# Group norm, attention and projection on one core: chains of the projections in row halves of the array, score units one at a time between their steps, products with v in lumps

## The chip, the core and the metric

The kernel runs on one core of a Trainium2 chip. The metric is the device time of one execution in microseconds (us): two runs of the kernel before gave 1596.97 and 1597.28, median 1597.12. The engines of the core are named as in its profile: PE (matrix multiply), PEld (its weight loads), DVE (vector), ACT (scalar, here mostly the exponential), POOL and SP (which issues most transfers). Each engine works through its own list in order; a wait in the list holds up everything behind it.

## What is computed

The input x is (4, 512, 48, 48): four batches (b), 512 channels, 2304 positions. The reference, cut to what matters (d is 64, 8 heads):

```python
hn = _group_norm(x, gn_scale, gn_bias)            # 32 groups
qkv = einsum('oc,bchw->bohw', qkv_w, hn) + qkv_b  # to float16, heads of 64
w = softmax(einsum('bhct,bhcs->bhts', q * scale, k * scale))
a = einsum('bhts,bhcs->bhct', w, v)
out = x + einsum('oc,bchw->bohw', proj_w, a) + proj_b
```

## The kernel before

Two heads of a batch form a pair; there are 16 pairs, g = 0 to 15. The 2304 queries are cut into five blocks j, four of 512 and one of 256. For one pair and block the work is a row of **score units**: a unit is k times q for 128 keys and 512 queries of both heads (two matmuls of 64 rows by 128 columns side by side in the two row halves of the array, one head each; line 1066), written to a slot of two PSUM banks, and one exponential of 128x1024 on ACT (L1073), which writes 16-bit numbers to SBUF. Three units are a step (BURST); there are 432 steps in all and 1296 units. The **product with v** (L1091) takes the exponentials two steps later: two matmuls of 128 rows by 64 columns, side by side in the two column halves, for each unit, summed in the PSUM bank av. DVE adds the exponentials of the steps up (L1122, L1127); PE sums them over the keys with a matrix of ones (sl, L1150), and the quotient goes through a small transfer to DRAM and back (L1169, L1197, L1207).

Beside this runs the rest of the work as **chains**, sums over the 512 channels in one PSUM bank that DVE empties at the end: pqk (q and k of coming pairs, L802, 32-bit, column halves), pv (v, L854, the same) and pr (output projection, L948, whole array, with weights split into a high and a low part). A 32-bit matmul appears in the trace as two instructions. The lists beside (chains waiting, each with the step at which it is needed) and fill (which after each step issues half a chain to a chain and a half, by how much must be done until when) set where chains stand. The main loop of fast_path writes, for each step: three score units, sums if a block ended, then chain pieces, then the product of the step two back. PSUM is split in three slots for scores, one bank for av and sl, one for chains.

Of the kernel before, what the change touches and what calls it, by code (L numbers as in the profile page):

```python
# [26 lines left out]
P = 128  # L27
# [6 lines left out]
BEHIND = 2  # L34
LAG = 2
# [435 lines left out]
def fast_path(  # L471
# [19 lines left out]
    apool = ctx.enter_context(tc.tile_pool(name="apool", bufs=2 * NPAIR - 1))  # L491
    ppool = ctx.enter_context(tc.tile_pool(name="ppool", bufs=3))
# [87 lines left out]
    share = const.tile([P, P // GROUP, GROUP], F32, name="share")  # L580
# [19 lines left out]
    def chain_bank(name):  # L600
        if alone[0]:
            return ps_s.tile([P, 2, QB], F32, tag="ps", name=name)[:, 0, :]
        return ps_w.tile([P, QB], F32, tag="pw", name=name)

    def small_bank(name):
        return ps_w.tile([P, QB], F32, tag="pw", name=name)
# [85 lines left out]
    def first_group(meanwhile):  # L692
# [5 lines left out]
        pv = ps_s.tile([P, 2, QB], F32, tag="ps", name="first_vars")[:, 0, 0:1]  # L698
# [59 lines left out]
    def piece(us, run, first=False, last=False, when=None):  # L758
        return [us, run, first, last, when, 0, NG]
# [16 lines left out]
    def idle_once(*engines):  # L776
        for engine in engines:
            if idle_left[engine] > 0:
                idle_left[engine] -= 1
                getattr(nc, engine).nop("place", nofuse=True)  # L780

# [47 lines left out]
    def qk_chain(g, part, j):  # L829
        n = QBLOCKS[j][1]  # L830
        steps = qk_steps(g, part, j)
        return chain_pieces(n / 600.0, steps, HALVES if n == QB else WHOLE)
# [4 lines left out]
    def v_chain(b, half, i):  # L837
# [31 lines left out]
        return chain_pieces(1.72, one, (range(1), range(1, 2)))  # L869
# [54 lines left out]
    def att32(b, j, pairs=range(NC), beside=None):  # L924
        o, n = QBLOCKS[j]
        for c in pairs:
# [10 lines left out]
            at32[b, j, c] = t[:, :n]  # L937
            source = atts[b * NPAIR + c][:, o : o + n]
# [45 lines left out]
    def proj_piece(b, j, chunks, pairs=range(NC), ahead=None):  # L984
        def run():
            evacuate, store = proj_run(b, j, chunks, pairs)
            evacuate()
            if pairs == LAST:
                finished.add((j, chunks[0]))

            if pairs != FIRST:
                loads.append((now[0] + 1, store))
            if ahead is not None:
                loads.append((now[0] + 1, ahead))

        return piece(QB / 290.0 * len(pairs) / NC, run, True, True)
# [55 lines left out]
    def scores(u, ahead_of_last=None):  # L1052
        g, j, k, _ = u
        o, n = QBLOCKS[j]
        per = QB // n
        qt, kt = qk[g]
        pt = ppool.tile([P, BURST, 2, QB], F16, tag="p", name=f"p_{g}_{j}_{k}")
        for r in range(BURST):
            if r == BURST - 1 and ahead_of_last:
                ahead_of_last()  # L1060
            ps = ps_s.tile([P, 2, QB], F32, tag="ps", name=f"ps_{g}_{j}_{k}_{r}")
            for a in range(per):
                i = (k * BURST + r) * per + a
                for h in range(2):
                    rows = slice(h * D, (h + 1) * D)
                    nc.tensor.matmul(  # L1066
                        ps[:, h, a * n : (a + 1) * n],
                        kt[rows, bass.ts(i, P)],
                        qt[rows, o : o + n],
                        start=True,  # L1070
                        stop=True,
                    )
            nc.scalar.activation(pt[:, r], ps, AF.Exp)  # L1073
        pts[u] = pt

    def values(u):
        g, j, k, last = u
        b, pr = divmod(g, NPAIR)
        o, n = QBLOCKS[j]
        per = QB // n  # L1080
        pt = pts.pop(u)
        if k == 0:
            if j == 0:
                atts[g] = apool.tile([P, T], F16, tag="att", name=f"att_{g}")
            av[0] = ps_av.tile([P, QB], F32, tag="av", name=f"av_{g}_{j}")
        for r in range(BURST):
            for a in range(per):
                i = (k * BURST + r) * per + a
                for h in range(2):
                    lo = h * D  # L1090
                    nc.tensor.matmul(  # L1091
                        av[0][lo : lo + D, :n],
                        vv[b, pr // 2][:, i, pr % 2 * P + lo : pr % 2 * P + lo + D],
                        pt[:, r, h, a * n : (a + 1) * n],
                        start=(i == 0),
                        stop=(i == NT - 1),
                    )
        if last and u is not stream[-1]:
            avx[g, j] = work.tile([P, QB], F32, tag="avx", name=f"avx_{g}_{j}")
            nc.vector.tensor_copy(avx[g, j][:, :n], av[0][:, :n])  # L1100
# [3 lines left out]
    def add(u):  # L1104

        g, j, k, last = u
        pt = pts[u]
        if k == 0:
            acc[g, j] = [pt]
            return  # L1110
        if j >= NQ - 2 and g == NG - 1 and (last or j == NQ - 1):
            acc[g, j].append(pt)
            return
        before = acc[g, j][0]
        if k == 1:
            acc[g, j] = [
                work.tile(
                    [P, BURST, 2, QB], F16, tag="acc", bufs=1, name=f"acc_{g}_{j}"
                )
            ]  # L1120
        t = acc[g, j][0]
        nc.vector.tensor_tensor(t, before, pt, ALU.add)  # L1122
        if last:
            acc[g, j] = [t[:, :1]]

            def join(r):
                nc.vector.tensor_tensor(t[:, 0], t[:, 0], t[:, r], ALU.add)  # L1127

            for r in range(1, BURST - 1):
                join(r)  # L1130
            joins.append(lambda: join(BURST - 1))

    def add_up(g, j, bank=None, more=False):
# [5 lines left out]
        if bank is None:  # L1139
            sl = ps_av.tile([P, QB], F32, tag="av", name=f"sl_{g}_{j}")  # L1140
        steps = [
            (t, r, a)
            for t in acc.pop((g, j))
            for r in range(t.shape[1])
            for a in range(per)
        ]
        for i, (t, r, a) in enumerate(steps):
            for h in range(2):
# [4 lines left out]
                    t[:, r, h, a * n : (a + 1) * n],  # L1153
# [58 lines left out]
    def divide(g, j):  # L1212
        divided[0] = now[0]
        o, n = QBLOCKS[j]
# [10 lines left out]
    def put(pieces, after=0, need=NG):  # L1225
        for p in pieces:
            p[5], p[6] = after, need
        beside.extend(pieces)

    def put_run(run, *args, when=None, after=0):  # L1230

        put([piece(0.05, lambda: run(*args), when=when)], after)

# [36 lines left out]
    def copies_next():  # L1270

        return any(p[0] == 0.0 and p[5] <= now[0] for p in beside[:2])

    def put_qk(g, part, blocks=range(NQ)):

        for j in blocks:
            put(qk_chain(g, part, j), (g - 2) * per_pair - 1, g)

    def put_v(b, half, tiles=range(0, NT, 2)):
        for i in tiles:  # L1280
            g = b * NPAIR + 2 * half
            pieces = v_chain(b, half, i)
            last = (b, i * P // QB, NC - 1)
            if half == 0:
                pieces[0][4] = lambda last=last: normed.get(last, now[0]) < now[0]
            put(pieces, (g - 2) * per_pair + 1, g)

    ends = [i for i, u in enumerate(stream) if u[3]]
    projs = {(b, j): proj_pieces(b, j) for b in range(B) for j in range(NQ)}

# [6 lines left out]
    def put_convert(b, j):  # L1297
        end = ends[((b + 1) * NPAIR - 1) * NQ + j]
        put(projs[b, j][0], end + ready(b, j))

    def put_proj(b, j, ahead=None):

        end = ends[((b + 1) * NPAIR - 1) * NQ + j]
        for p in projs[b, j][1]:
            if ahead:
                put_run(*ahead.pop(0))
            put([p], end + ready(b, j) + 1)

    def put_first(b, j, ahead):

        for jj, chunks in proj_list:
            if jj == j:
                if ahead:
                    put_run(*ahead.pop(0))
                put([proj_piece(b, j, chunks, FIRST)])

    for b in range(B):
        g = b * NPAIR
        old = b - 1
        if b == 0:  # L1320
            for j in range(NQ):
# [4 lines left out]
                put_qk(g + 1, 1, (j,))  # L1326
                put_qk(g + 1, 0, (j,))
            for block in SPARE:
                put_run(reload, *block)
        put_qk(g + 2, 1)  # L1330
        put_qk(g + 2, 0)
# [6 lines left out]
        if b == B - 1:  # L1338
            put_qk(g + 3, 1)
            put_qk(g + 3, 0, range(NQ - 1))  # L1340
            put_convert(old, 0)
            put_qk(g + 3, 0, (NQ - 1,))

            THIRD = range(len(EARLY), NC - 1)
            ahead = [
                (residual, b, j, chunks)
                for j in (NQ - 2, NQ - 3, NQ - 1)
                for jj, chunks in proj_list
                if jj == j
            ]  # L1350
            ahead += [
                (att32, b, j, (c,)) for j in (NQ - 2, NQ - 3, NQ - 1) for c in EARLY
            ]
            ahead.append((att32, b, NQ - 2, THIRD))
            for j in range(NQ):
                put_proj(old, j, ahead)
                if j + 1 < NQ:
                    put_convert(old, j + 1)
            assert not ahead

            ahead = [
                (att32, b, NQ - 3, THIRD),
                (att32, b, NQ - 1, THIRD),
                *((att32, b, 0, (c,), True) for c in EARLY),
            ]
            for j in (NQ - 2, NQ - 3, NQ - 1):
                put_first(b, j, ahead if j != NQ - 2 else [])
# [8 lines left out]
        for j in early:  # L1376
            if j == NQ - 1 and b > 0:
                put_convert(old, 0)
            put_qk(g + 3, 1, (j,))
            put_qk(g + 3, 0, (j,))  # L1380
            put_run(reload, b + 1, j)
        for j in late:
            put_v(b, 1, tiles[j])
            put_qk(g + 3, 1, (j,))
            put_qk(g + 3, 0, (j,))
        if b > 0:
            for j in range(NQ - 1):
                put_proj(old, j)
                put_convert(old, j + 1)
        put_v(b + 1, 0)  # L1390
        if b > 0:
            put_proj(old, NQ - 1)
        put_qk(g + 4, 1)
        put_qk(g + 4, 0)
        put_qk(g + 5, 1)
        put_qk(g + 5, 0)
# [305 lines left out]
```

## Time and profile before

| | us |
|---|---|
| median of the two runs | 1597.12 |
| span of the profiled execution, first to last instruction | 1595.6 |
| PE busy | 1582.0 (99%) |
| ACT busy | 1269.4 (80%) |
| DVE busy | 1140.2 (71%) |

The page gives for the profiled execution the span of its instructions; the median of the runs lies 1.5 us above it. A group's row reads: line, engine, operation, tile written <- tiles read, shape, count | busy time in all, mean ns of one | idle time before them. Matmuls are pipelined: one lasts longer than the distance to the next, so distances between starts are read from the timeline, and a PE that shows as busy all the time may still lose time in switching between halves.

### The profile page before, as it was taken

How to read it: one execution, taken by the hardware profiler on the slowest of the kernel's cores; microseconds unless marked ns; L12 is line 12 of the kernel's file. 1: busy time of each engine (PE TensorE's matmuls, PEld its weight loads, DVE VectorE, ACT ScalarE, POOL GpSimd, SP SyncE). 2: the span in 40 equal slices, each digit the busy share in tenths (PEclk: the TensorE clock that was granted, in tenths of full speed). 3: DMA queues.
4: the chain of work that ended last, by engine and by line, in shares of the span. 5: the costliest groups of instructions: out<-in, count | busy, mean ns of one | idle time of the engine just before them, and what ended most of it. 6: DMA issues, size and time to landing. Idle time of an engine off the chain costs nothing. (4 is left out here: it accounts for less than half of the span.)

```text
span 1595.6 us, 28731 instructions
## 1 busy us (share of the span) xinstructions
PE 1582.0 (99%) x11526; PEld 701.7 (44%) x11526; DVE 1140.2 (71%) x1302; ACT 1269.4 (80%) x1363; POOL 336.8 (21%) x463
## 2 busy tenths in 40 slices
PE   9999999999999999999999999999999999999997
PEld 3733434443333534545333354455533334434554
DVE  6267668876666678887666666888767676767776
ACT  4177777888888888888888888887878888888885
POOL 1001202222121222312112121222212121121232
PEclk9999999999999999999999999999999999999999
DMA  7002020000000024521000001353101000015424
GB/s 222 3 14 67 12 73 16 18 14 12 15 18 11 12 69 119 144 67 28 11 14 18 14 12 41 111 158 88 23 17 18 15 15 11 15 31 166 149 62 133
DMA packets 94896, 82.10 MB, mean 51 GB/s; under 512 B 50852, under 2 KB 60964, under 8 KB 94756
## 3 DMA queue, kind: packets, MB, share of 16 engines
q1 hardware_dynamic: 92724, 78.35, 18.1%
q8 instruction: 92, 1.51, 0.4%
q10 hardware_dynamic: 1904, 1.84, 0.4%
q14 instruction: 48, 0.39, 0.1%
q0 software_dynamic: 128, 0.01, 0.0%
HBM read 60.70 MB, written 19.17 MB: 50 GB/s over the span
## 5 line engine op out<-in xcount | busy, mean ns | idle before, releaser
L1073 ACT ACTIVATE p<-ps 128x1024 f16<-128x1024 f32 x1296 | 1233.5, 1025 | 299.1 <-PE ps L1066 296.3
L1122 DVE TENSOR_TENSOR acc<-acc,p 128x3072 f16<-128x3072 f16 x270 | 485.4, 1798 | 53.8 <-ACT p L1073 51.3
L802 PE MATMUL pqk<-x,wqkv 128*64 128x512 f32 (+1 forms) x2432 | 510.3, 549 | 0.1
L1091 PE MATMUL av<-p,v 128*64 128x512 f16 (+1 forms) x2880 | 360.6, 364 | 0.0
L1066 PE MATMUL ps<-q,k 64*128 64x512 f16 (+1 forms) x2880 | 355.8, 358 | 0.4 <-DVE v L862 0.2
L854 PE MATMUL pv<-wqkv,x 128*64 128x256 f32 x2304 | 267.6, 379 | 0.3 <-DVE v L862 0.3
L802 PEld LDWEIGHTS pqk<-x,wqkv 128*64 128x64 f32 x2432 | 168.5, 137 | 205.4 <-issue 155.9
L1188 POOL TENSOR_SCALAR in<-sums 128x8 f32<-128x8 f32 (+1 forms) x158 | 100.8, 638 | 712.4 <-DMA sums<-slx 705.8
L1066 PEld LDWEIGHTS <-k 64*128 64x128 f16 x2880 | 105.9, 94 | 287.2 <-issue 238.2
L1091 PEld LDWEIGHTS <-v 128*64 128x64 f16 x2880 | 131.2, 109 | 212.8 <-issue 168.1
L1215 POOL TENSOR_TENSOR att<-avx,ib 128x512 f16<-128x512 f32 (+1 forms) x78 | 133.1, 1706 | 422.9 <-DMA ib<-row 373.7
L854 PEld LDWEIGHTS pv<-wqkv,x 128*64 128x64 f32 x2304 | 166.3, 137 | 81.3 <-DVE v L862 0.8
L1122 DVE TENSOR_TENSOR acc<-p,p 128x3072 f16<-128x3072 f16 x79 | 138.1, 1748 | 0.0
L948 PE MATMUL pr<-a,whi 128*128 128x512 f32 (+1 forms) x311 | 121.8, 399 | 0.1
L1127 DVE TENSOR_TENSOR acc<-acc 128x1024 f16<-128x1024 f16 x156 | 114.7, 735 | 3.3
L948 PE MATMUL pr<-a,wlo 128*128 128x512 f32 (+1 forms) x311 | 113.5, 372 | 0.0
L813 DVE TENSOR_SCALAR q<-pqk,bqkv 128x512 f16<-128x512 f32 (+1 forms) x77 | 53.5, 694 | 76.0 <-PE pqk L802 75.5
L813 DVE TENSOR_SCALAR k<-pqk,bqkv 128x512 f16<-128x512 f32 (+1 forms) x75 | 52.2, 695 | 77.7 <-PE pqk L802 77.5
L862 DVE TENSOR_TENSOR v<-pv,bv 128x512 f16<-128x512 f32 x72 | 49.7, 690 | 79.6 <-PE pv L854 79.5
L1166 DVE COPY slx<-sl 128x512 f32<-128x512 f32 (+1 forms) x79 | 50.6, 641 | 64.1 <-PE sl L1150 64.1
L975 DVE SCALAR_TENSOR_TENSOR r<-pr,bproj,r 128x512 f32<-128x512 f32 (+1 forms) x80 | 54.9, 695 | 41.3 <-PE pr L948 36.6
L1100 DVE COPY avx<-av 128x512 f32<-128x512 f32 (+1 forms) x79 | 50.6, 640 | 36.4 <-PE av L1091 36.1
(124 smaller groups left out, 506.7 us busy)
## 6 DMA issues: line engine op xcount, KB each, us to landing
r<-x_dram SPq DMA_DIRECT2D x72, 256.0 KB, 3.6
out_dram<-r SPq DMA_DIRECT2D x69, 256.0 KB, 2.4
ib<-row SPq DMA_DIRECT2D x126, 128.0 KB, 3.1
x<-x_dram SPq DMA_DIRECT2D x62, 256.0 KB, 3.9
x<-x_dram SPq DMA_DIRECT2D x16, 128.0 KB, 4.8
sums<-slx SPq DMA_DIRECT2D x128, 2.0 KB, 2.1
ib<-row SPq DMA_DIRECT2D x30, 64.0 KB, 3.0
wqkv<-qkv_wT_dram SPq DMA_DIRECT2D x2, 768.0 KB, 6.9
```

Of the source, the lines that this page charges most:

```text
L802: nc.tensor.matmul(pw[0][lo : lo + D, :n], wqkv[:, c, w0 + lo : w0 + lo + D], hn[b, c, j], start=(c == 0), stop=(c == NC - 1),)
L813: nc.vector.tensor_scalar(qk[g][part][:, o : o + n], pw[0][:, :n], bqkv[:, col : col + 1], SCALE, ALU.add, ALU.mult,)
L854: nc.tensor.matmul(pw[0][lo : lo + D, a, :], hn[b, c, i * P // QB][:, at + lo : at + lo + D], wqkv[:, c, 2 * C + half * C // 2 :][:, : C / ...
L948: nc.tensor.matmul(ps[:, :n], w[:, c, bass.ts(m, P)], at32[b, j, c], start=(i == 0), stop=(i == len(steps) - 1),)
L975: nc.vector.scalar_tensor_tensor(xt[:, i], places[i], bias, xt[:, i], ALU.add, ALU.add)
L1066: nc.tensor.matmul(ps[:, h, a * n : (a + 1) * n], kt[rows, bass.ts(i, P)], qt[rows, o : o + n], start=True, stop=True,)
L1073: nc.scalar.activation(pt[:, r], ps, AF.Exp)
L1091: nc.tensor.matmul(av[0][lo : lo + D, :n], vv[b, pr // 2][:, i, pr % 2 * P + lo : pr % 2 * P + lo + D], pt[:, r, h, a * n : (a + 1) * n], ...
L1122: nc.vector.tensor_tensor(t, before, pt, ALU.add)
L1127: nc.vector.tensor_tensor(t[:, 0], t[:, 0], t[:, r], ALU.add)
L1188: nc.gpsimd.tensor_scalar(t, sm, limit, None, op)
L1215: nc.gpsimd.tensor_tensor(atts[g][:, o : o + n], avx.pop((g, j))[:, :n], ibs.pop((g, j))[:, :n], ALU.mult,)
```

## The change

Steps 0 to 422 of 432 (HANDED) are no longer written by the loop but by row_phase, a function that runs while the program is built. It keeps a clock for PE, ACT and DVE with the durations of the table US and chooses at each point what PE gets next; the built program holds only the chosen order, with its semaphores.

Chains become objects (Chain) that are started two at a time (Pair). A pair takes one of the three slots, its two banks one for each chain. A step of it is two matmuls side by side: channels 0 to 63 of a chunk for the one chain in the upper row half, channels 64 to 127 for the other in the lower; after all chunks the halves are exchanged. Between the two halves (mark) the pair waits until a product with v of a unit scored after the mark has been issued. Score units are the same two matmuls as before, but each is issued by itself, into the slot that the clock says is free first, and while a pair is open two slots are left. The products with v are collected and issued in a lump, either when nothing else may go, or to let a pair exchange its halves. av and sl take the two remaining banks in turn (y_bank).

The exponentials go to one ring of 12 places instead of three tiles of a step; a step that runs over the end of the ring is added by DVE in two parts, and the sum of a block takes a place in the ring too. A batch of projections now waits in a list of its own (lane) until its inputs are converted. The last 9 steps run in the old loop. The attended tiles have six instead of seven buffers.

```diff
+RING = 12
+PAIRED = 77
+HANDED = 423
...
+US = {
+    "unit": 0.216,
+    "exp": 0.955,
+    "hand": 0.08,
+    "switch": 0.097,
+    "add": 1.8,
+    "join": 0.735,
+    "copy": 0.64,
+    "out": 0.695,
+}
...
-    ppool = ctx.enter_context(tc.tile_pool(name="ppool", bufs=3))
+    ppool = ctx.enter_context(tc.tile_pool(name="ppool", bufs=1))
...
-    ps_s = ctx.enter_context(tc.tile_pool(name="ps_s", bufs=3, space=PSUM))
-    ps_av = ctx.enter_context(tc.tile_pool(name="ps_av", bufs=1, space=PSUM))
-    ps_w = ctx.enter_context(tc.tile_pool(name="ps_w", bufs=1, space=PSUM))
+    banks = ctx.enter_context(tc.tile_pool(name="banks", bufs=1, space=PSUM))
...
+    def slot(name, i=None):
...
+        return banks.tile([P, 2, QB], F32, tag=f"s{i}", name=name)
+    def y_bank(name, i):
+        return banks.tile([P, QB], F32, tag=f"y{i % 2}", name=name)
...
+        def op(c, r):
+            rows = slice(r * D, (r + 1) * D)
...
+                nc.tensor.matmul(
+                    bank[:, :n],
+                    wqkv[rows, c, w0 : w0 + P],
+                    hn[b, c, j][rows],
+                    start=start,
+                    stop=stop,
+                )
...
+    ring = ppool.tile([P, RING, 2, QB], F16, tag="p", name="ring")
...
+    def turn_of(n, r):
+
+        return n * BURST + r + blocks_before[n]
+
+    def place(n, r):
+        return turn_of(n, r) % RING
...
+    def score_unit(n, r, i=None):
...
+        ps = slot(f"ps_{g}_{j}_{k}_{r}", i)
...
+        nc.scalar.activation(ring[:, place(n, r)], ps, AF.Exp)
...
+            (t,) = acc[g, j]
+            for lo, hi, p in segments(n):
+                nc.vector.tensor_tensor(
+                    t[:, lo:hi], t[:, lo:hi], ring[:, p : p + hi - lo], ALU.add
+                )
+        if last:
+            total = ring[:, place(n, BURST)]
...
+    def score():
+        n, r = units[scored[0]]
+        i = free.index(min(free))
+        stall("score", free[i])
...
+        score_unit(n, r, i)
+        spent(US["unit"], True)
+        clock["act"] = max(clock["act"], clock["pe"]) + US["exp"]
+        free[i] = clock["act"] + US["hand"]
...
+        done_exp[scored[0]] = clock["act"] + US["hand"]
+        scored[0] += 1
...
+    def sum_up():
...
+            if g * NQ + j < HANDED_BLOCK:
+                event(t + 2.6, inverted)
...
+        stall("value", done_exp[valued[0]])
...
+    def lump(through=-1):
+        if clock["row"]:
+            spent(0.0, False)
+        while valued[0] < min(scored[0], (HANDED - BEHIND) * BURST) and (
+            valued[0] <= through or done_exp[valued[0]] <= clock["pe"] + 0.02
+        ):
+            value()
+            if sums_ready():
...
+    class Pair:
+        def __init__(self, first, second, queue):
...
+            self.slot = free.index(min(free))
+            stall("pair", free[self.slot])
+            advance(clock["pe"])
+            free[self.slot] = math.inf
+            self.tile = slot(f"pair_{names[0]}", self.slot)
...
+            self.halves = [
+                list(zip(sides[0](h), sides[1](1 - h))) for h in range(2)
+            ]
+            self.half, self.at, self.mark = 0, 0, None
...
+            half = self.halves[self.half]
...
+            for (us, emit), bank in zip(half[self.at], range(2)):
+                emit(self.tile[:, bank, :], first, last)
...
+            if self.at == len(half):
+                if self.half == 0:
+                    self.half, self.at, self.mark = 1, 0, scored[0]
...
+    def row_phase():
...
+            now_p = pair[0]
+            if now_p and now_p.waits():
+                if swap_now():
+                    now_p.mark = None
...
+            if c_ok and s_ok:
+                soon_free = sum(x <= t + 0.4 for x in free)
+                if not now_p and soon_free < 2:
+                    s_ok = False
+                elif clock["act"] < t + LEAD:
+                    c_ok = False
...
+            if s_ok:
+                score()
+            elif c_ok:
+                if now_p:
+                    now_p.step()
+                else:
...
-    for n in range(end):
+    row_phase()
+    handed[0] = True
...
+    for n in range(HANDED, end):
```

**The order at three places.** What PE does next after a product with v, at pair 7, block 0. In the rows, ps_g_j_k_r is the score of pair g, block j, step k, unit r; av is the product with v, pair_n a pair of chains, L1276, L1299 and L889 the lines of score, product and chain step after the change. Before:

```order
L1066 LDWEIGHTS k_7_5862
L1066 MATMUL ps_7_0_0_1_7719<-q_7_5861,k_7_5862 128x512
L1066 LDWEIGHTS k_7_5862
L1066 MATMUL ps_7_0_0_1_7719<-q_7_5861,k_7_5862 128x512
L1066 LDWEIGHTS k_7_5862
L1066 MATMUL ps_7_0_0_2_7723<-q_7_5861,k_7_5862 128x512
L1066 LDWEIGHTS k_7_5862
L1066 MATMUL ps_7_0_0_2_7723<-q_7_5861,k_7_5862 128x512
L1091 LDWEIGHTS v1_1_5236
L1091 MATMUL av_6_4_7701<-p_6_4_1_7627,v1_1_5236 64x256
```

The change, at the same units:

```order
L1276 LDWEIGHTS k_7_5532
L1276 MATMUL ps_7_0_0_1_7601<-q_7_5531,k_7_5532 128x512
L1276 LDWEIGHTS k_7_5532
L1276 MATMUL ps_7_0_0_1_7601<-q_7_5531,k_7_5532 128x512
L889 MATMUL pair_63_7503<-x_2_0_2_5854,wqkv_94 128x512 x2
L1276 LDWEIGHTS k_7_5532
L1276 MATMUL ps_7_0_0_2_7607<-q_7_5531,k_7_5532 128x512
L1276 LDWEIGHTS k_7_5532
L1276 MATMUL ps_7_0_0_2_7607<-q_7_5531,k_7_5532 128x512
L889 MATMUL pair_63_7503<-x_2_1_2_5856,wqkv_94 128x512 x2
```

Before, the third unit followed the second at once into a third slot, and the column-half product came next. Now a chain step stands between them, all in row halves, and the third unit takes the slot of the first, since the pair holds the third slot.

The second place is PE's list at pair 10, block 1. Before, each step there had a projection chain (pr) ahead of its scores:

```order
L948 MATMUL pr_1_1_1_10890<-a32_1_1_3_10810,whi_154 128x512
L948 MATMUL pr_1_1_1_10890<-a32_1_1_3_10810,wlo_155 128x512
L1066 LDWEIGHTS k_10_8915
L1066 MATMUL ps_10_1_4_0_10904<-q_10_8914,k_10_8915 128x512
L1066 LDWEIGHTS k_10_8915
L1066 MATMUL ps_10_1_4_0_10904<-q_10_8914,k_10_8915 128x512
```

The change:

```order
L1276 LDWEIGHTS k_10_8585
L1276 MATMUL ps_10_1_4_2_10926<-q_10_8584,k_10_8585 128x512
L1276 LDWEIGHTS k_10_8585
L1276 MATMUL ps_10_1_4_2_10926<-q_10_8584,k_10_8585 128x512
L1276 LDWEIGHTS k_10_8585
L1276 MATMUL ps_10_1_5_0_10941<-q_10_8584,k_10_8585 128x512
L1276 LDWEIGHTS k_10_8585
L1276 MATMUL ps_10_1_5_0_10941<-q_10_8584,k_10_8585 128x512
L1299 LDWEIGHTS v1_2_9138
L1299 MATMUL av_10_1_10847<-ring_166,v1_2_9138 64x512
```

For 39 units here no chain step stands in the list: two units and two products alternate.

The third place is pair 0, block 3, just after a lump; the product in the last row reads the exponential of the unit ps_0_3_3_2 (the pair waits there for its exchange):

```order
L1276 LDWEIGHTS k_0_264
L1276 MATMUL ps_0_3_3_2_1406<-q_0_263,k_0_264 128x512
L1276 LDWEIGHTS k_0_264
L1276 MATMUL ps_0_3_3_2_1406<-q_0_263,k_0_264 128x512
L1276 LDWEIGHTS k_0_264
L1276 MATMUL ps_0_3_4_0_1413<-q_0_263,k_0_264 128x512
L1276 LDWEIGHTS k_0_264
L1276 MATMUL ps_0_3_4_0_1413<-q_0_263,k_0_264 128x512
L1299 LDWEIGHTS v0_0_507
L1299 MATMUL av_0_3_1311<-ring_166,v0_0_507 64x512
```

Before, the product that followed a score read exponentials two steps old; here it reads that of the unit but one ahead of it.

More of the change, by code (lines that the diff above doesn't have):

```diff
@@ L1139, in add_up @@
         if bank is None:
[L1140 to L1147, printed above, removed]
+            sl = y_bank(f"sl_{g}_{j}", side(g, j))
+        steps = []
+        for t in acc.pop((g, j)):
+            if isinstance(t, int):
+                units = [ring[:, place(t, r)] for r in range(BURST)]
+            else:
+                units = [t[:, r] for r in range(t.shape[1])]
+            steps += [(t, a) for t in units for a in range(per)]
+        for i, (t, a) in enumerate(steps):
             for h in range(2):
@@ new lines, in fast_path, with spent @@
+    free = [0.0] * 3
+    units = [(n, r) for n in range(HANDED) for r in range(BURST)]
+    done_exp, ended_av = {}, {}
+    scored, valued, added = [0], [0], [-1]
+    summing = deque()
+    rowed, added_up = set(), set()
+    summed_at = {}
+    owed = [0.0, 0.0]
+    names = [0]
+    trace = []
+    def spent(us, row):
+        if DEBUG:
+            trace.append((clock["pe"], us, row, pair[0] and (pair[0].half, pair[0].at)))
+        t = clock["pe"]
+        if clock["row"] != row:
+            t += US["switch"]
+            counts["switch"] = counts.get("switch", 0) + 1
+            clock["row"] = row
+        clock["pe"] = t + us
```

933 lines of the change are left out of this document (780 added, 153 removed).

## Prediction

> **What bounds the kernel now.** I read the page first: who is busy, and whether that changes over the span.
>
> ```profile
> span 1595.6 us, 28731 instructions
> PE 1582.0 (99%) x11526; PEld 701.7 (44%) x11526; DVE 1140.2 (71%) x1302; ACT 1269.4 (80%) x1363; POOL 336.8 (21%) x463
> PE   9999999999999999999999999999999999999997
> ACT  4177777888888888888888888887878888888885
> PEclk9999999999999999999999999999999999999999
> L1073 ACT ACTIVATE p<-ps 128x1024 f16<-128x1024 f32 x1296 | 1233.5, 1025 | 299.1 <-PE ps L1066 296.3
> ```
>
> PE is busy in every slice at full clock; ACT has a fifth free, and its idle time ends at PE's scores. So PE's list is the bound. Next the waits of PE itself:
>
> ```profile
> PE count L1641 <- DVE good L1640: 2.3, 1, 2.3
> PE ps L1066 <- DVE v L862: 0.2, 1, 0.2
> ```
>
> PE waits for next to nothing, so the list runs back to back, and only what it does counts. The timeline of PE shows that:
>
> ```profile
> 800.33 0.82 PE L1066 MATMUL ps<-q,k 64*128 64x512 f16 x6
> 801.08 0.84 PE L1091 MATMUL av<-p,v 128*64 128x512 f16 x6
> 801.75 1.88 PE L802 MATMUL pqk<-x,wqkv 128*64 128x512 f32 x8
> 803.57 0.82 PE L1066 MATMUL ps<-q,k 64*128 64x512 f16 x6
> 804.32 0.84 PE L1091 MATMUL av<-p,v 128*64 128x512 f16 x6
> 804.99 1.89 PE L802 MATMUL pqk<-x,wqkv 128*64 128x256 f32 x16
> 806.82 0.82 PE L1066 MATMUL ps<-q,k 64*128 64x512 f16 x6
> 807.57 0.84 PE L1091 MATMUL av<-p,v 128*64 128x512 f16 x6
> 808.24 3.60 PE L802 MATMUL pqk<-x,wqkv 128*64 128x512 f32 x16
> 811.77 0.39 PE L1066 MATMUL ps<-q,k 64*128 64x512 f16 x2
> ```
>
> One pair of score matmuls lasts 0.39; three pairs 0.82, so pairs start (0.82 - 0.39) / 2 = 0.215 apart. A unit of score or of product costs PE 0.215. But the product starts 0.75 after the three units' start, not 0.645: going from row to column halves costs 0.105. From product to chain it is 0.67, 0.025 more than 0.645. Eight chain matmuls take 1.82 up to the next scores, sixteen 3.53: eight cost 1.71 in themselves, and the way back to row halves 0.11. One change of halves is so (0.105 + 0.025 + 0.11) / 2 = 0.12. Projections use the whole array:
>
> ```profile
> 668.40 0.84 PE L1091 MATMUL av<-p,v 128*64 128x512 f16 x6
> 669.17 0.50 PE L948 MATMUL pr<-a,whi 128*128 128x512 f32 x1
> 669.50 0.39 PE L948 MATMUL pr<-a,wlo 128*128 128x512 f32 x1
> 669.73 0.40 PE L948 MATMUL pr<-a,whi 128*128 128x512 f32 x1
> 669.97 0.39 PE L948 MATMUL pr<-a,wlo 128*128 128x512 f32 x1
> 670.90 0.40 PE L948 MATMUL pr<-a,wlo 128*128 128x512 f32 x1
> 671.23 0.82 PE L1066 MATMUL ps<-q,k 64*128 64x512 f16 x6
> ```
>
> They start 0.235 apart, the first takes 0.33, and the way out 0.10.
>
> **What the change saves on PE.** Counted over PE's whole list, the mode of the array changes 955 times before and 496 times after: 459 x 0.12 = 55 us less. The whole array is entered 76 times before, 16 after: 60 x 0.10 = 6. The 384 projection steps of 512 now run in row halves; at 0.215 as scores do they save 384 x 0.02 = 8, at the old 0.235 nothing; I take 4. The chain matmuls are as many as before and stream the same columns; no row shows 32-bit ones in row halves. Low bound for a pass of 256 columns: what column halves take, (1.83 - 0.11) / 8 = 0.215 from the row of sixteen. High bound: 0.235, as in the whole array with loads of 128 columns. I take 0.215, the nearer, since scores in row halves also keep 0.215. Sum: 65 us less PE work.
>
> **What it adds: the loop through ACT.** Before, a slot is used again after a whole step, over 3 us later, and ACT is never in PE's way. Now the first place of the order puts the third unit into the slot of the first after two units and a chain step: 2 x 0.215 + 0.855 (half of 1.71) = 1.285. What must lie between is seen at the start of the span, where PE once did wait for a slot:
>
> ```profile
> 75.70 0.82 PE L1066 MATMUL ps<-q,k 64*128 64x512 f16 x6
> 76.13 4.69 ACT L1073 ACTIVATE p<-ps 128x1024 f16<-128x1024 f32 x5 [0.19 <-PE ps L1066]
> 78.32 1.11 PE L1066 MATMUL ps<-q,k 64*128 64x512 f16 x6
> 79.04 0.09 PEld L1066 LDWEIGHTS <-k 64*128 64x128 f16 x1 [0.40 <-issue]
> 675.25 1.02 ACT L1073 ACTIVATE p<-ps 128x1024 f16<-128x1024 f32 x1 [0.54 <-PE ps L1066]
> ```
>
> ACT starts 0.43 after PE's matmul does (75.70, 76.13). One exponential lasts 1.02; five take 4.69, so they follow each other at (4.69 - 1.02) / 4 = 0.917. The third ends at 76.13 + 2 x 0.917 + 1.02 = 78.98, and at 79.04 PE's third unit of the next step, which needs its slot, goes on; its step lasts 1.11 instead of 0.82. So the loop is 0.43 + 1.02 + 0.05 = **1.50**. The table that laid out the order counts 0.216 + 0.955 + 0.08 = 1.25. Three waits follow, each counted by going along PE's list with the prices above, a wait moving all that is behind it.
>
> Slots: at 272 places outside the chainless stretches below, the slot's last unit lies less than 1.50 back, mostly at 1.285 and 0.21 short; mean 0.19: **52 us**. Nothing hides it, as the chain steps behind the waiting unit stand in the same list. Lower bound: with a loop of 1.25, 6 us.
>
> Chainless stretches (second place of the order): 120 units in seven stretches, the longest of 39 and 30, have no chain step between them. PE's work there is 63 us, ACT's 120 x 0.917 = 110. Of the 47 over, each stretch hides about one unit in free slots, 7 x 0.92: **40 us**. Before, every step had chain work, which covered ACT.
>
> Products (third place): at 45 places a lump ends with a unit whose exponential isn't done. At nineteen it stands two units and a change of halves behind the score, 2 x 0.215 + 0.12 = 0.55, so 0.95 is missing: 18 us; the other 26 are small: together **23 us**, with a loop of 1.25 some 14.
>
> DVE adds in 70 more instructions, since the ring cuts steps:
>
> ```profile
> L1122 DVE TENSOR_TENSOR acc<-acc,p 128x3072 f16<-128x3072 f16 x270 | 485.4, 1798 | 53.8 <-ACT p L1073 51.3
> L1127 DVE TENSOR_TENSOR acc<-acc 128x1024 f16<-128x1024 f16 x156 | 114.7, 735 | 3.3
> sums<-slx SPq DMA_DIRECT2D x128, 2.0 KB, 2.1
> ```
>
> 3072 cost 1798 and 1024 cost 735, so 1024 elements are 0.53 and an instruction's fixed part 0.20: 70 x 0.20 = 14 us on an engine that is idle 29% of the time. I count it at nothing; that idle time is its cover, and 14 us is the price without it.
>
> Sum against the profiled span: 1595.6 - 65 + 52 + 40 + 23 = 1645.6; with the 1.5 between span and median, **1647 us**.
>
> **The rivals.** *The loop is short* (not slower). If a slot comes back after 1.25, or the waits fall together with PE being late anyway, slots cost 6 and products 14, and ACT bounds only the chainless stretches: 1595.6 + 1.5 - 65 + 6 + 40 + 14 = 1592, down to about 1557 if the stretches too are half covered (-20) and the projections and entries save 15 more. Against it: the 1.11 row above, a wait of just this kind. It decides from a loop under 1.3. Chance 0.33, a third of it below 1565.
>
> *Loads of 128 columns bound the chains in row halves* (slower still). The rows for weights:
>
> ```profile
> L802 PEld LDWEIGHTS pqk<-x,wqkv 128*64 128x64 f32 x2432 | 168.5, 137 | 205.4 <-issue 155.9
> L1066 PEld LDWEIGHTS <-k 64*128 64x128 f16 x2880 | 105.9, 94 | 287.2 <-issue 238.2
> L948 PEld LDWEIGHTS pr<-a,wlo 128*128 128x128 f32 x311 | 58.6, 188 | 7.9
> L1091 PEld LDWEIGHTS <-v 128*64 128x64 f16 x2880 | 131.2, 109 | 212.8 <-issue 168.1
> ```
>
> A 32-bit load of 64 columns takes 137 ns, one of 128 takes 188. If that makes each pass start 0.235 after the last as in the projections, the 2208 chain matmuls, two passes each and two side by side, pay 2208 x 0.02 = 44: 1691. Against it: 188 fits into 215, and the loads run beside the matmuls. Chance 0.15. The Trainium skill, "TensorE: Matmul & The Clock Gate", section "LDWEIGHTS (loading the stationary operand)", has the time of a load go by its columns alone, whatever the rows; by that rule the 64-row loads of the chains cost as much as the 128-row ones of pr, which is this rival's premise. The trace agrees for 32 bits, 137 and 188 ns; for 16 bits it doesn't, where 128 columns of k take 94 and 64 columns of v 109.
>
> *DVE stands behind transfers.* The inverse of the sums stands in DVE's list a planned 2.6 after the copy (event in the diff); the first of two transfers lands 2.1 after its issue. If DVE reaches it early, it holds the emptying of pairs behind it: 79 blocks x 0.4 = 32: 1679. Against it: DVE has work of its own in most of that time. Chance 0.07.
>
> **How the numbers follow.** Forecast 0.45, short loop 0.33, loads 0.15, DVE 0.07. A measurement tells about 2% (32 us) from no change: faster is below 1565, slower above 1629. Faster: a third of the short loop, 0.11. Slower: loads and DVE, and nine tenths of the forecast, whose own spread is 1615 to 1680: 0.62. The rest, 0.27, lies within 2%. The range leaves out the short loop's lowest and the loads' top end: 1570 to 1702.
>
> **What would show each step.** PE's waits, next to nothing now, should name ACT p (now the ring) before ps for some 90 us and before av for some 20; ps starts should show 0.2 idle after a lump's second unit; around two thirds of the span a stretch of 39 units should run at ACT's 0.92. Changes of halves should cost the same 0.12. The prediction is wrong if PE's waits for ACT stay under 40 us, or if chain steps of 512 columns start more than 0.9 apart.

## The result: 6.7% slower

The changed kernel takes **1704.5 us** (median of 1704.0 to 1704.9) against 1597.1 before: a ratio of 1.067, 95% interval 1.064 to 1.070. The forecast was 1647, range 1570 to 1702: the direction came, 57 us of the size did not. The profiled execution spans 1702.3 us, and its page reads:

```profile
span 1702.3 us, 30571 instructions
PE 1607.5 (94%) x12030; PEld 903.9 (53%) x12030; DVE 1144.1 (67%) x1372; ACT 1279.9 (75%) x1368; POOL 289.5 (17%) x458
PE   9999999999989999699999999988999999999887
ACT  4277776877778877287778788788878777868885
PEclk9999999999999999899999999999999999999999
L1283 ACT ACTIVATE ring<-ps 128x1024 f16<-128x1024 f32 x1296 | 1243.0, 1041 | 377.1 <-PE ps L1276 366.5
```

PE is no longer full in every slice, and ACT has become emptier (75%, not 80%) although PE now waits for it. Neither engine is the bound all the time; they wait for each other in turn. PE's own waits:

```profile
PE ps L1276 <- ACT ring L1283: 29.9, 62, 2.4
PE av L1299 <- ACT ring L1283: 16.4, 26, 0.9
PE pair L1134 <- DVE r L1107: 9.4, 2, 7.4
PE ps L1276 <- DVE r L1155: 3.6, 3, 3.2
PE pr L1080 <- DVE r L1107: 2.6, 1, 2.6
```

This view shows only a part. A matmul of 512 columns is recorded for 0.38 us but gives way to the next after 0.215, so the first 0.17 of every wait is hidden in the record. The whole is found by going along the starts of PE's list: from each distance the streaming of the step is taken off (0.215 for a unit, 0.43 for one of the two passes of a chain step of 512 columns), then up to 0.108 where the array changes halves; what is left over 0.025 is a wait, put down to the engine whose semaphore came last, or to "other gaps" where no engine's did. The sums, in us, with those of the experiments below (8.6 to 9.6 before the first and behind the last step are not in it). The time is the median of all runs, the sums are those of the profiled execution, which lies within 2 us of it but for exp_half (1615.1):

| kernel | time | streaming | changes (count) | other gaps | waits for ACT | for DVE, POOL |
|---|---|---|---|---|---|---|
| before | 1597.1 | 1464.1 | 91.8 (954) | 24.7 | 0.3 | 6.1 |
| changed | 1704.5 | 1455.8 | 51.7 (496) | 37.0 | 118.7 | 29.5 |
| exp_half | 1611.1 | 1457.3 | 49.4 (494) | 34.3 | 18.8 | 44.2 |
| exp_3q | 1629.6 | 1455.8 | 50.7 (494) | 32.6 | 42.1 | 37.6 |
| no_res | 1684.2 | 1455.8 | 51.7 (496) | 29.8 | 121.7 | 14.8 |
| half_no_res | 1594.0 | 1455.8 | 49.3 (494) | 29.8 | 19.5 | 26.8 |
| hand33 | 1692.9 | 1456.3 | 59.4 (577) | 35.9 | 102.7 | 27.4 |
| h20 | 1693.2 | 1455.2 | 54.9 (530) | 46.1 | 95.7 | 31.0 |
| loop112 | 1754.9 | 1455.9 | 50.9 (488) | 41.5 | 158.8 | 37.0 |
| before_mid | 1676.7 | 1464.1 | 157.5 (1592) | 40.9 | 0.0 | 3.8 |

From before to changed: PE's own list is 8.3 + 40.1 - 12.3 = 36 us shorter, the waits for ACT add 118, those for DVE 23: +106 against 106.7 between the spans.

The waits for ACT are of three kinds. One is between chain steps, where the time from a unit's start until its slot is free (the loop) counts; PE's timeline, then ACT's:

```profile
306.33 0.61 PE L1276 MATMUL ps<-q,k 64*128 64x512 f16 x4
306.76 1.04 PE L966 MATMUL pair<-wqkv,x 64*128 64x256 f32 x8
307.84 0.39 PE L1276 MATMUL ps<-q,k 64*128 64x512 f16 x2
```

```profile
306.76 3.77 ACT L1283 ACTIVATE ring<-ps 128x1024 f16<-128x1024 f32 x4 [0.49 <-PE ps L1276]
```

Two units, then four pairs of passes of 0.215: 306.76 + 0.86 = 307.62. The third unit comes at 307.84, 0.22 late. Its slot is that of the unit at 306.33, whose exponential starts at 306.76 and lasts 1.02: 307.78, and 0.05 for the way back. It is the loop of 1.50 against a distance of 1.285, as forecast; 216 such waits make 47.5 us. The second kind is in stretches of four and more units without a chain step:

```profile
1136.88 10.35 ACT L1283 ACTIVATE ring<-ps 128x1024 f16<-128x1024 f32 x11
1140.86 0.39 PE L1276 MATMUL ps<-q,k 64*128 64x512 f16 x2 [0.52 <-ACT ring L1283]
1141.19 0.62 PE L1299 MATMUL av<-ring,v 128*64 128x512 f16 x4
1141.78 0.39 PE L1276 MATMUL ps<-q,k 64*128 64x512 f16 x2
1142.70 0.39 PE L1276 MATMUL ps<-q,k 64*128 64x512 f16 x2 [0.52 <-ACT ring L1283]
```

Eleven exponentials without a break, (10.35 - 1.02) / 10 = 0.93 apart, and for two units PE has nothing else to do than two products (four matmuls): 40.9 us. Products at the end of a lump make the third kind: 22.7 us in 48 places.

The waits for DVE are fewer, and some are long. The largest, first in PE's and then in DVE's timeline:

```profile
701.85 0.40 PE L1080 MATMUL pr<-a,wlo 128*128 128x512 f32 x1
709.64 0.58 PE L1134 MATMUL pair<-a,whi 64*128 64x256 f32 x2 [7.40 <-DVE r L1107]
```

```profile
704.67 0.74 DVE L1155 SCALAR_TENSOR_TENSOR r<-pair,bproj,r 128x512 f32<-128x512 f32 x1
708.75 0.75 DVE L1107 SCALAR_TENSOR_TENSOR r<-pr,bproj,r 128x512 f32<-128x512 f32 x1 [3.33 <-DMA r<-x_dram]
```

and SP's:

```profile
705.44 0.34 SPq L1170 DMA_DIRECT2D out_dram<-r  x1
705.83 0.42 SPq L1036 DMA_DIRECT2D r<-x_dram  x1
```

A projection chain (pr) ends at 702.25, but DVE empties it by adding the residual x, and this x is only asked for at 705.83, behind the store of the tile emptied at 704.67. It lands 2.9 later; until then the slot is not free, and the next pair waits 7.4. In all, DVE waits 25.9 us in seven places for such loads; in the kernel before it waits for none of them.

Of what the prediction named as signs, those of ACT's loop came: waits before scores and products, units 0.92 apart around two thirds of the span. Neither sign of its being wrong came: the waits for ACT are far over 40 us, and chain steps of 512 columns start 0.86 apart.

### The profile page after: what moved, and what is told of

The parts are those of the page before. It is cut to its first block, busy times and chain, and to the rows that moved or that the text cites. A ratio compares the mean times of both kernels' runs of the same rounds, so it can differ in the third digit from the quotient of the medians.

```text
span 1702.3 us, 30571 instructions
## 1 busy us (share of the span) xinstructions
PE 1607.5 (94%) x12030; PEld 903.9 (53%) x12030; DVE 1144.1 (67%) x1372; ACT 1279.9 (75%) x1368; POOL 289.5 (17%) x458
## 5 line engine op out<-in xcount | busy, mean ns | idle before, releaser
L1283 ACT ACTIVATE ring<-ps 128x1024 f16<-128x1024 f32 x1296 | 1243.0, 1041 | 377.1 <-PE ps L1276 366.5
L1354 DVE TENSOR_TENSOR acc<-acc,ring 128x3072 f16<-128x3072 f16 (+2 forms) x315 | 490.2, 1563 | 238.3 <-ACT ring L1283 236.4
L889 PE MATMUL pair<-x,wqkv 64*128 64x512 f32 (+1 forms) x2400 | 548.6, 549 | 1.6 <-ACT ring L1283 0.7
L1276 PE MATMUL ps<-q,k 64*128 64x512 f16 (+1 forms) x2880 | 481.9, 360 | 47.1 <-ACT ring L1283 29.9
L1276 PEld LDWEIGHTS <-k 64*128 64x128 f16 x2880 | 177.2, 94 | 398.4 <-issue 377.3
L1299 PE MATMUL av<-ring,v 128*64 128x512 f16 (+1 forms) x2880 | 346.4, 364 | 18.5 <-ACT ring L1283 16.4
L889 PEld LDWEIGHTS pair<-x,wqkv 64*128 64x128 f32 x2400 | 233.6, 187 | 97.7 <-issue 54.1
L966 PE MATMUL pair<-wqkv,x 64*128 64x256 f32 x2016 | 267.6, 379 | 1.1 <-ACT ring L1283 0.5
L1299 PEld LDWEIGHTS <-v 128*64 128x64 f16 x2880 | 154.9, 110 | 181.9 <-issue 98.9
L966 PEld LDWEIGHTS pair<-wqkv,x 64*128 64x128 f32 x2016 | 197.4, 188 | 29.9 <-ACT ring L1283 3.7
L1344 DVE TENSOR_TENSOR acc<-ring 128x3072 f16<-128x3072 f16 (+2 forms) x104 | 141.3, 1369 | 77.3 <-ACT ring L1283 77.2
L1134 PE MATMUL pair<-a,whi 64*128 64x512 f32 (+1 forms) x504 | 110.1, 435 | 10.8 <-DVE r L1107 9.4
```

Source lines behind the costliest of these rows:

```text
L889: nc.tensor.matmul(bank[:, :n], wqkv[rows, c, w0 : w0 + P], hn[b, c, j][rows], start=start, stop=stop,)
L966: nc.tensor.matmul(bank.rearrange("p (a n) -> p a n", a=2)[:, at, :], hn[b, c, i * P // QB][rows, t0 : t0 + P], wqkv[rows, c, 2 * C + half ...
L1134: nc.tensor.matmul(bank[:, at * n : (at + 1) * n], w[rows, c, bass.ts(m, P)], at32[b, j, c][rows], start=start, stop=stop,)
L1276: nc.tensor.matmul(ps[:, h, a * width : (a + 1) * width], kt[rows, bass.ts(i, P)], qt[rows, o : o + width], start=True, stop=True,)
L1283: nc.scalar.activation(ring[:, place(n, r)], ps, AF.Exp)
L1299: nc.tensor.matmul(av[0][lo : lo + D, :width], vv[b, pr // 2][:, i, pr % 2 * P + lo : pr % 2 * P + lo + D], ring[:, place(n, r), h, a * wi ...
```

## The experiments

**Take ACT's loop away, all of it and by a quarter.** exp_half lets the exponential take one head's half; its readers read that half twice. before_half is the same in the kernel before.

```diff
-        nc.scalar.activation(ring[:, place(n, r)], ps, AF.Exp)
+        nc.scalar.activation(ring[:, place(n, r), 0], ps[:, 0], AF.Exp)
...
-                    ring[:, place(n, r), h, a * width : (a + 1) * width],
+                    ring[:, place(n, r), 0, a * width : (a + 1) * width],
```

> The changed kernel with its order as it is, but the exponential takes only one of the two heads' halves (512 of 1024 columns), and products and sums read that half for both heads: the other half of the exponentials is left out. ACT's loop and cadence are then about half as long. Theory A (ACT's loop is the loss): the 118.7 us that PE waits for ACT in the trace of the changed kernel go, the rest stays: 1704.5 - 118.7 = 1586. Rival B (ACT's waits hide waits for DVE behind them): PE's waits for DVE grow from 29 to some 65, and the time is about 1620. Rival C (the loss is in PE's own list, and the waits for ACT are only its shadow): above 1680.

> The kernel before with the same half of the exponentials left out. Before, PE waits for ACT 0.3 us in all, so every theory has it at 1597 +- 5. What it is for is the difference to the changed kernel with half exponentials, in which neither waits for ACT: by the prediction's own terms (PE saves 65, DVE costs nothing) the changed one is then 65 us faster; by the two traces (changes of halves 40, streaming 8, other gaps of PE 12 given back, waits for DVE 24 more) it is 12 us faster; where the waits for DVE grow (rival B) it is 20 us slower.

exp_half took 1611.1 (ratio to before 1.008, 1.006 to 1.010), before_half 1597.1 (1.000, 0.999 to 1.001). ACT's group row and PE's first waits in exp_half:

```profile
L1283 ACT ACTIVATE ring<-ps 128x512 f16<-128x512 f32 x1296 | 745.2, 597 | 775.5 <-PE ps L1276 752.7
```

```profile
PE sl L1390 <- DVE ring L1366: 8.9, 3, 5.3
PE pair L1134 <- DVE r L1107: 8.5, 2, 6.0
PE av L1299 <- ACT ring L1283: 6.4, 14, 0.5
```

The exponential falls to 0.597, the loop to 0.43 + 0.60 + 0.05 = 1.08, below the distance of 1.285, and 93 of the 107 us go: C falls. A's 118.7 is not reached: waits for ACT lose 100, those for DVE and POOL rise by 15 (now DVE stands first in the list), as B has it to a part. With most of ACT's waits gone, the new order is still 14 us behind the old one.

exp_3q cuts the exponential to 768 columns, so that the loop is just what the order's table takes it for.

```diff
-        nc.scalar.activation(ring[:, place(n, r)], ps, AF.Exp)
...
+            ring[:, place(n, r)].rearrange("p h q -> p (h q)")[:, :768],
+            ps.rearrange("p h q -> p (h q)")[:, :768],
...
```

> The changed kernel in the same order with an exponential of 768 of the 1024 columns (products and sums read some columns twice, the rest is left out). The loop is then 0.43 + some 0.80 + 0.05 = 1.28, about what the table of the order takes it for, and units follow each other at some 0.70. Theory A (the prediction's arithmetic by distances: the loop against the 1.285 between a slot's last unit and its next): slot waits 47 go to about 3, stretches without chains 37 to about 15, products 23 to 14; 1704.5 - 75 = 1629, and up to 10 more for waits on DVE that come out from behind: 1629 to 1639. Rival B (PE loses in proportion to ACT's work, whatever the distances): half way between 1704 and 1611, 1657.

It took 1629.6 (1.020, 1.019 to 1.022): A, to the microsecond of its lower end. The row of ACT:

```profile
L1298 ACT ACTIVATE ring<-ps 128x768 f16<-128x768 f32 x1296 | 994.1, 816 | 548.0 <-PE ps L1291 535.3
```

0.43 + 0.82 + 0.05 = 1.30. The waits between chain steps fall from 47.5 to 7.4 us, those in the stretches from 40.9 to 19.3, those of products from 22.7 to 12.4; DVE's rise by 8. A quarter of an exponential takes four fifths of what a half takes: between chain steps the size of the loop against the distance decides, not ACT's amount of work. In the stretches without chains ACT's pace counts, and there the quarter takes about half.

**Take the waits for the residual away.** no_res neither loads nor adds x (but for the last blocks), half_no_res does this in exp_half.

```diff
-        nc.sync.dma_start(xt, rows_of(x, b, j, chunks))
+        if in_two(b, j):
+            nc.sync.dma_start(xt, rows_of(x, b, j, chunks))
...
+                    nc.vector.tensor_scalar(xt[:, i], source, bias, None, ALU.add)
```

> The changed kernel in the same order, without the residual (x is neither loaded for it nor added, but for the last three blocks of the last batch): DVE's emptying of a projection then waits for no load of x. Theory A (DVE stands behind the loads of the residual, 25.9 us in seven places, and PE behind DVE, 9.4 + 4.3 + 2.6 + 1.0 = 17 us in eight): 1704.5 - 17 = 1687. Rival (PE's next slot comes from ACT anyway, so that what DVE gives back is waited for at ACT): above 1698.

> The changed kernel in the same order, with half of the exponentials left out (as in exp_half, 1611) and without the residual (as in no_res, 20 us less than the changed kernel). If the two losses add up: 1611 - 20 = 1591, which would be the first order of this kind under the 1597 of before: what PE saves in its own list (36 to 44 us by the traces) then stands against some 35 of waits left. If the residual only mattered because ACT was late too: 1605 to 1611.

no_res took 1684.2 (1.054, 1.052 to 1.056), 20 us less: A, and 3 more than its 17. DVE is busy for as long as in the changed kernel (1143.9 us against 1144.1), so beside the loads themselves only its waits went. Among PE's longest waits there is no row with r any more:

```profile
PE ps L1279 <- ACT ring L1286: 31.9, 65, 2.4
PE av L1302 <- ACT ring L1286: 16.2, 25, 0.9
PE count L2506 <- DVE good L2505: 2.3, 1, 2.3
```

By the table, waits for DVE lose 15 and other gaps 7 (waits for ACT gain 3). The 7 lie in stretches in which PE ran at half its clock (last section): about 11.5 us of the changed kernel's other gaps lie there, about 4 in no_res. half_no_res took 1594.0 (0.998, 0.997 to 0.999), 17 us less than exp_half: the two losses add up but for 3 us. With both gone, the order by pairs is 3 us ahead of the one by steps: its list is 46 us shorter (1455.8 + 49.3 + 29.8 against 1464.1 + 91.8 + 24.7), and 40 of them go into waits that are left (46.3 against 6.4). The kernel before was not run without the residual, so the 3 us are no fair lead; its DVE waits for no load of it.

**The transfers of the sums and the cut adds.** no_inv takes the inverse from a constant, so that DVE stands behind no transfer of sums; before_cut splits every add in the kernel before.

```diff
-        nc.vector.reciprocal(inv[:, :, :per], sums[g, j][:, :, :per])
+        one = ones.unsqueeze(2).to_broadcast((P, 2, per))
+        nc.vector.reciprocal(inv[:, :, :per], one)
```

```diff
-        nc.vector.tensor_tensor(t, before, pt, ALU.add)
+        for part in (slice(0, 1), slice(1, BURST)):
+            nc.vector.tensor_tensor(t[:, part], before[:, part], pt[:, part], ALU.add)
```

> The changed kernel in the same order, with the inverse of the sums taken from a constant and not from what the transfer of the sums brings (the division by the sums is left out; all transfers and instructions stay). DVE then no longer stands 27.1 us in 32 places behind these transfers. Theory A (the prediction's rival: DVE held behind transfers holds the emptying of pairs and with it PE): PE's waits for DVE fall by most of that, 1704.5 - 20 to 27, so 1677 to 1684. Rival B (these places fall where neither a slot nor a sum is due; of PE's 29 us of waits for DVE only those behind loads of the residual are real): 1700 to 1705.

> The kernel before with each of its some 350 adds of 3072 elements cut into two (1024 and 2048), the same sums otherwise. At 0.20 for an instruction's fixed part DVE has 70 us more to do, five times what the ring's 70 more adds bring. Theory A (the prediction: DVE's idle time covers it): 1597 to 1600. Rival B (adds stand ahead of the emptying of chains and are paid in full): 1597 + 70 = 1667; a tenth of it, 1604, would still price the ring's adds at 1.4 us.

no_inv took 1703.6 (1.066, 1.064 to 1.068), as much as the changed kernel: B. PE's waits for r stand as they were:

```profile
PE pair L1134 <- DVE r L1107: 8.0, 2, 5.9
PE ps L1276 <- DVE r L1155: 2.9, 3, 2.4
```

So DVE can stand 27 us behind the sums at no price and 26 us behind the residual at 20. The likely reason is whether a slot hangs on the instruction; but the waits differ in length too (27.1 us in 32 places, 25.9 in seven), and no run separates the two. before_cut took 1598.6 (1.000, 0.999 to 1.001): A, with 349 more instructions on DVE, busy for 33.5 us more by its record, 0.10 each and not the prediction's 0.20:

```profile
PE 1582.7 (99%) x11526; PEld 701.8 (44%) x11526; DVE 1173.7 (73%) x1651; ACT 1269.6 (79%) x1363; POOL 301.7 (19%) x463
```

**Change the loop in the table.** hand33 plans with the measured loop, h20 with one between, loop112 with one too short.

```diff
-    "hand": 0.08,
+    "hand": 0.33,
```

```diff
-    "hand": 0.08,
+    "hand": 0.20,
```

```diff
-    "exp": 0.955,
-    "hand": 0.08,
+    "exp": 0.85,
+    "hand": 0.05,
```

> The changed kernel with one number of its table corrected: what lies between the end of an exponential and the slot being free goes from 0.08 to 0.33, so that the loop that lays out the order is the measured 1.50. Theory A (the prediction's: the order puts units too close since its loop is too short): the slot waits outside the stretches without chains, 52 by the prediction, and some 9 of the waits before products go: 1704.5 - 61 = 1643. Rival B (while a pair of chains is open it holds one of three slots, scores go round two; chain work put into the gaps is used up sooner, and the stretches without chains grow by what the gaps lose): the waits only move, 1690 to 1715, with PE's waits for ACT still above 95.

> The changed kernel with the return of the slot at 0.20 in its table, so that the order is laid out for a loop of 1.37, between the 1.25 that it has (1704) and the measured 1.50 (1693). Theory A (a trade: a longer loop in the table takes waits from between chain steps and gives them to the stretches without chains, so that the best lies in between): 1680 to 1692, changes of halves about 530, waits for ACT about 95. Rival B (the time falls steadily with the error of the table): 1697 to 1700.

> The changed kernel with its table made worse on purpose: exponential 0.85 and return of the slot 0.05 instead of 0.955 and 0.08, so that the order is laid out for a loop of 1.12 where 1.50 is measured (the table of the changed kernel has 1.25). Theory A (waits only move: what the slots lose between chain steps, the stretches without chains give back, as with the loop of 1.50 in the table): 1692 to 1716. Rival B (beyond some point nothing is given back: every one of the 270 places that fall short falls short by 0.13 more): 1704.5 + 35 = 1740.

Waits for ACT by kind, in us, from the starts of PE's steps:

| loop in the table | time | between chain steps | stretches without chains | products | other |
|---|---|---|---|---|---|
| 1.12 (loop112) | 1754.9 | 66.3 | 43.3 | 33.0 | 16.2 |
| 1.25 (changed) | 1704.5 | 47.5 | 40.9 | 22.7 | 7.6 |
| 1.37 (h20) | 1693.2 | 18.7 | 49.4 | 20.4 | 7.2 |
| 1.50 (hand33) | 1692.9 | 10.4 | 70.3 | 14.9 | 7.1 |

hand33 (1.060, 1.058 to 1.062): B. The waits between chain steps go, as A says; but a unit that is put off leaves its place to a chain step, the chains are used up sooner, and the stretches grow by 29. One of them is 88 us long, with ACT busy for all but 1.5 us and PE for three quarters; the columns are the stretch, its length, and busy time (instructions) of PE, PEld, DVE, ACT and POOL, then clock, share of transfers and GB/s:

```profile
1488.00:1576.00 88.00, 64.15 (x426) 20.88 (x422) 60.79 (x59) 86.49 (x99) 24.15 (x30) 0.94 0.13 33
```

There are also 81 changes of halves more. h20 (1.060, 1.058 to 1.062) lies 1 us above A's range, with A's counts: flat between 1.37 and 1.50, no dip. loop112 (1.099, 1.097 to 1.100) lies above both: nothing is given back on that side. But B's mechanism makes only a part of its 50 us: between chain steps 19 come and not 35, the rest before products (10), at other places (9), for DVE (7.5) and in small amounts elsewhere. Of the tables tried, the best is worth 12 us.

**The price of a change of halves.** before_mid moves the products of a step ahead of its third unit.

```diff
+        mid = n >= BEHIND and not (inside or summed or n - BEHIND - 1 in soon)
+        early = (lambda: values(stream[n - BEHIND])) if inside or mid else None
+        scores(stream[n], early)
```

> The kernel before with the three products of a step moved ahead of its third score unit (not where a block of sums or the end is near). Its list of PE is the same but for the order: the mode of the array changes 1593 times, not 955, and eight products' ways out lead into column halves or the whole array as before. Theory A (the prediction's price, 0.12 a change, which is the whole way round divided by two): 638 x 0.12 = 77: 1597 + 77 = 1674. Rival B (the price read from all changes of the trace, 91.8 us over 954, so 0.096; what the prediction added, 0.025 between product and chain, is no change of halves): 638 x 0.096 = 61: 1658. Both say that PE still waits for ACT under 3 us in all.

It took 1676.7 (1.050, 1.048 to 1.051): 79.4 us for 638 changes, **0.124 each**. A. Its timeline shows where that lies:

```profile
800.34 0.61 PE L1066 MATMUL ps<-q,k 64*128 64x512 f16 x4
800.88 0.84 PE L1091 MATMUL av<-p,v 128*64 128x512 f16 x6
801.65 0.39 PE L1066 MATMUL ps<-q,k 64*128 64x512 f16 x2
801.97 3.65 PE L802 MATMUL pqk<-x,wqkv 128*64 128x512 f32 x16
805.56 0.61 PE L1066 MATMUL ps<-q,k 64*128 64x512 f16 x4
```

Two units take 0.54 instead of 0.43, three products 0.77 instead of 0.645, a unit 0.32 instead of 0.215, and the chain 3.59, 0.06 more than before. The change itself is 0.10; the rest is lost within the products or the chain behind it.

## Why the prediction was wrong, step by step

- **PE saves 65**: the step is right in kind and mis-sized, 36 in the changed kernel and 46 in half_no_res. The price of 0.12 was read from one place and holds for changes that are added there (0.124). But over the whole list before, the 954 changes hold 91.8 us and the products 8.8 behind them, 0.105 each, so that there was less to save than 955 x 0.12. Changes, product steps behind them and first steps of projections together fall from 108.5 (91.8 + 8.8 + 7.9) to 61.5 (51.7 + 5.3 + 4.5): 47, where 61 stood. The projections gain 2, not 4, since their steps start 0.23 apart in row halves too. The rest, 13, was given back in other gaps, which the prediction didn't have; about 11.5 us of such gaps lie in stretches at half clock, and the kernel before has no such stretch but at its end.
- **Slot waits 52**: 47.5, in 216 places and not 272, at 0.22 and not 0.19 each. Loop and distance are as worked out; exp_3q shows that the loop decides.
- **Chainless stretches 40**: 40.9. **Products 23**: 22.7.
- **DVE at nothing**: this is the step that failed in its mechanism. For adds it holds in the kernel before (before_cut); in the changed order it was not tried. But in the sum DVE stood for its adds alone. Its emptying of projection chains was never put beside the loads of the residual: in the new order a chain can end before its load is even asked for (by 3.6 us in the place shown), and the load takes another 2.9. This costs 20 us with the clock; the other 9 us of DVE's waits were not traced further. The rival "DVE stands behind transfers" had the mechanism, with a chance of 0.07, and the wrong transfer.
- **Loads of 128 columns** did not bound the chains: passes of 256 columns start 0.215 apart, steps of 512 columns 0.86. **The short loop** would have ended at 1592 by the forecast; exp_3q, with a loop of 1.30, ends at 1630, although its stretches without chains cost only 19: the waits for DVE and the smaller saving of PE stay.

What was missing from +50 to +107 is so 29 of PE's saving, 23 for DVE, 3 for ACT and 1 ahead of the first and behind the last step. Not shown, only argued: why distances come out at 1.285. In the order 1098 of the 1296 units are scored while a pair is open, that is with two slots; an order with a fourth slot was not tried.

## What to carry to other kernels

A buffer that is lent to another stage shortens the distance to its next use: compare that distance with the whole loop through the other engine (0.43 + 1.02 + 0.05 here, not the 1.02). Work that fills a gap is missing later; a planner that fills every wait with it moves the wait to where that work has run out. And an instruction that gives a buffer back must not stand behind a transfer that was issued after the work it ends.

## What the chip showed beside this

A long wait of PE can be paid a second time. Behind the 7.4 us, in the stretch 709.6 to 713.6, the granted clock was 0.56, then 1.00:

```profile
709.60:713.60 4.00, 3.88 (x34) 3.71 (x36) 0.56 (x1) 0.00 (x0) 0.00 (x0) 0.56 0.73 239
713.70:715.40 1.70, 1.70 (x32) 1.68 (x29) 0.62 (x1) 0.00 (x0) 0.00 (x0) 1.00 0.14 48
```

The passes of 256 columns, 0.12 apart at full clock, stood 0.215 apart for these 4 us. The same came behind a wait of 2.7 us up to 669.2 (0.55 for 3.3 us). The Trainium skill, "TensorE: Matmul & The Clock Gate", section "Part 1: The HAM clock gate (the "warmup" mystery)", has the clock halved after an idle window of about 3.4 us and given back after as long a busy one. The trace agrees at the 7.4 us, where the clock falls about 4 us after the wait begins and comes back about 3.5 us after PE goes on. It agrees less elsewhere: 2.7 us were enough at 669, and in one stretch without chains the clock fell although no wait of PE was over 0.7 us (0.82 in the mean), while in another of the same kind it stayed full:

```profile
1127.00:1161.00 34.00, 25.16 (x162) 7.58 (x159) 32.73 (x51) 34.00 (x39) 6.75 (x8) 1.00 0.14 45
1555.00:1583.00 28.00, 22.39 (x128) 6.13 (x126) 19.09 (x18) 28.00 (x35) 7.86 (x10) 0.82 0.31 76
```

What makes the difference stays open. In the kernel before, PE never waits over 2.3 us, and its clock shows nothing of it until the last 4 us.
